# Selective scans of a four-layer vision model: where the scanned states lie, and which engine multiplies them with C

## The chip, the cores and the metric

The kernel runs on one core of a Trainium2 chip. A core has five engines that work at the same time and wait for each other through semaphores: TensorE (PE; its weight loads are listed as PEld), VectorE (DVE), ScalarE (ACT), GpSimd (POOL) and SyncE (SP), which issues the DMAs here. There are two on-chip memories, SBUF and PSUM. The metric is device time in microseconds for one execution of the whole program.

## The reference

The model has four layers on images of 64 x 64 pixels with 96 channels, batch 4. Layers 0 and 1 are state-space blocks; layers 2 and 3 are attention and feed-forward layers on tokens, and play only a side part here. The core of both blocks is a selective scan, done in four directions over the image:

```python
def step(hst, inputs):
    ul, dl, bl, cl = inputs
    dA = jnp.exp(dl[..., None] * A)
    hst = hst * dA + (dl * ul)[..., None] * bl[:, :, None, :]
    y = jnp.einsum('bkdn,bkn->bkd', hst, cl)
    return (hst, y)
h0 = jnp.zeros(u_l.shape[1:] + (A.shape[-1],), u.dtype)
_, ys = jax.lax.scan(step, h0, (u_l, delta_l, B_l, C_l))
```

For each channel there are 16 states n. Each state follows h = exp(delta A) h + (delta u) B along the sequence, and y is the sum over the 16 states of h times C. Around the scan, block 0 has a projection, a 3 x 3 depthwise convolution and SiLU before it, and a normalisation, a gate and an output projection after it; block 1 has the same between a two-dimensional Fourier transform and its inverse.

## The kernel before

**Tiling.** 128 partitions hold channels and the free dimension holds positions. The 192 channels of two images (block 0) or the 384 channels of one image (block 1) make three chunks, c = 0, 1, 2. There are six phases: two of block 0 (two images each) and four of block 1 (one image each). A phase goes through the four directions, each cut into segments: eight of 512 positions in block 0; 512, 512, 384, 384 and 320 in block 1. That makes 64 + 80 = 144 segments.

**Steps.** A segment is done in 12 steps: four quarters q of the 16 states, and in each quarter the three chunks. A step (class `Step`) scans four states, numbered j = 0 to 3 in the quarter. There are 1728 steps, listed in `steps`, and one loop (`for i, st in enumerate(steps)`) writes the instructions of all engines for a step. `tc.manual_schedule(engines=IN_ORDER)` makes TensorE, VectorE, ScalarE and GpSimd keep the order in which this loop writes them; so what stands behind a waiting instruction on its engine waits too.

**What a step needs.** For each of its four states a scan takes a factor exp(delta A) and an addend (delta u) B:

- States 0 and 1: the factors are written by ScalarE into the SBUF tile `ax` (`front_x`, line 635 through `exp`). The addends come from `bx`, which ScalarE makes with positions on the partitions (line 600, `make_bx`, given out in pieces by `Pieces.take`), and which TensorE transposes into PSUM (`transposed`, line 630).
- States 2 and 3: the factors are written by ScalarE into PSUM (`front_y`, line 635; these lines of the profile call the tile `ab`, `b` or `_l`, which is a matter of shortened names). The addends are made in SBUF by GpSimd as a product of `du` and a row of B (`front_b`, line 653).
- The PSUM tiles of both kinds come from one ring of three banks (`room`, tag `ab`).

VectorE scans (line 660). States 0 and 1 go to the SBUF tile `hx`; states 2 and 3 are scanned in place in the SBUF tile `hy`, of which there is one buffer. Each scan reads one tile in SBUF and one in PSUM. GpSimd multiplies the two states of `hx` with C in one instruction (`hcx`, line 805), VectorE those of `hy` (`hcy`, line 822). TensorE transposes each product by a matmul with the identity and adds it into a PSUM bank for the chunk (`accumulate`, line 682; 16 such matmuls a step at 512 positions), so that the sum over the 16 states is done there. After the last quarter `close_chunk` (line 709) copies the sum out and stores it.

The last column of each state is kept as the start value for the next segment (`keep_state`, line 673): for `hx` on GpSimd behind the multiply, for `hy` mostly on ScalarE.

**Loads.** The rows of B and C are broadcast over the partitions by DMAs (`broadcast`, line 580). `fetch` loads a quarter ahead, in the first chunk's step: two C tiles of two rows each from a ring of four buffers, and one B tile of two rows from a ring of two.

**Other work in the gaps.** While one segment is scanned, the next is prepared (`prepare`, with one VectorE product `du`, line 560, per segment), and the work of the other layers and images runs as generators on a queue (`Env`), some pieces per step, through `slot`. `burst` marks the places where ScalarE changes its function table (softplus, SiLU). VectorE's and GpSimd's order in a step is:

```python
scan x0; scan x1; scan y0; scan y1; hcy          # VectorE
hcx; copy of two columns; du*B for y0'; du*B for y1'   # GpSimd, ' is the next step
```

Of the kernel before, what the change touches and what calls it, by code (L numbers as in the profile page):

```python
# [456 lines left out]
class Seg:  # L457


    def __init__(self, ph, k, a, S, first, last):  # L460
# [8 lines left out]
        self.bx, self.b, self.c, self.u, self.after = {}, {}, {}, None, None  # L469


class Step:


    def __init__(self, z, q, c):
        self.z, self.q, self.c = z, q, c
        self.nm = f"{z.nm}_{q}_{c}"


def scans(tc, ctx, phases, ident):  # L480
# [92 lines left out]
    def broadcast(z, n, what):  # L573
# [3 lines left out]
        t = sp.tile([P, 2, SM], F32, name=f"bc{what}_{z.nm}_{n}", tag=f"bc{what}", bufs=2 + 2 * what)  # L577
        for i in range(NI):
            r = i * cfg.M + cfg.R + what * NST + n
            nc.sync.dma_start(  # L580
                out=t[i * PI : (i + 1) * PI, :, :S],
                in_=z.xd[r : r + 2, :S].rearrange("(o n) l -> o n l", o=1).to_broadcast([PI, 2, S]),
            )
        return t

    def fetch(z, q):
        z.c[q] = [broadcast(z, 4 * q + 2 * j, 1) for j in range(2)]
        z.b[q] = broadcast(z, 4 * q + 2, 0)
# [37 lines left out]
    def transposed(st, j):  # L626

        pb = room(st, j)
        for b, (t, n) in enumerate(st.z.blocks):
            nc.tensor.transpose(pb[:, t : t + n], st.z.bx[st.q, j][:n, b, st.c], ident[:n, :n])  # L630
        return pb
# [12 lines left out]
    def front_y(st, j):  # L644
        st.ay[j] = room(st, 2 + j)
        exp(st.ay[j][:, : st.z.S], st, 4 * st.q + 2 + j)

    def front_b(st):

        S = st.z.S  # L650
        st.hy = sp.tile([P, 2, SM], F32, name=f"hy_{st.nm}", tag="hy")
        for j in range(2):
            nc.gpsimd.tensor_tensor(  # L653
                st.hy[:, j, :S], st.z.du[:, st.c, :S], st.z.b[st.q][:, j, :S], ALU.mult
            )

    def scan(st, h, j, a, b, n):
        z = st.z
        step = -1 if z.rev else 1
        nc.vector.tensor_tensor_scan(  # L660
            h[:, j, : z.S][:, ::step],
            a[:, : z.S][:, ::step],
            b[:, : z.S][:, ::step],
# [5 lines left out]
    def keep_state(copy, st, h, n0):  # L669
        z = st.z  # L670
        if not z.last:
            e = 0 if z.rev else z.S - 1
            copy(  # L673
                z.state[st.c][:, n0 : n0 + 2].rearrange("p (j o) -> p j o", o=1), h[:, :, e : e + 1]
            )

    def accumulate(st, hc, n0):
        z = st.z
        for j in range(2):
            blocks = list(enumerate(z.blocks))  # L680
            for b, (t, n) in blocks[:: 1 - 2 * j]:
                nc.tensor.matmul(  # L682
                    z.acc[st.c][:n, b, :],
                    hc[:, j, t : t + n],
                    ident,
                    start=(n0 + j == 0 and b == 0),
                    stop=(n0 + j == NST - 1 and b == 0),
                    is_transpose=True,
                )

    def open_segment(z, before):
# [5 lines left out]
        else:  # L697
            z.state = before.state
        z.acc = [
            ps.tile([P, 512], F32, name=f"acc_{z.nm}_{c}", tag=f"acc{c}").rearrange("p (b d) -> p b d", b=NBK)  # L700
            for c in range(C)
        ]
# [17 lines left out]
    with tc.manual_schedule(engines=IN_ORDER):  # L720
        drain(prepare(segs[0]))
        drain(make_bx(segs[0], 0))
        fetch(segs[0], 0)
        st = steps[0]
        st.px, st.ay = [transposed(st, j) for j in range(2)], {}
        front_x(st)
        front_b(st)
        front_y(st, 0)
        closing = None
# [33 lines left out]
        for i, st in enumerate(steps):  # L763
            z, q, c, S = st.z, st.q, st.c, st.z.S
            nxt = steps[i + 1] if i + 1 < len(steps) else None
            if q == 0 and c == 0:
                after = z.after
                if at == 0 or z.ph is not segs[at - 1].ph:
                    if closing:
                        close_chunk(closing)  # L770
                        closing = None
# [725 lines left out]
```

## Time and profile before

| What | Value |
|---|---|
| Median of 3 runs | 11709.09 us (11697.75 to 11709.36) |
| Span of the profiled execution | 11704.4 us |
| Before the first scan | 0 to 215.5 us |
| Two phases of block 0 | 2551.9 and 2585.7 us |
| Four phases of block 1 | 1469.7, 1446.8, 1521.8 and 1516.9 us |
| Behind the last scan | 396.1 us |
| VectorE busy in these eight stretches | 111, 2420, 2436, 1306, 1295, 1427, 1410 and 143 us |
| GpSimd busy | 5, 2264, 2214, 1143, 1146, 1080, 1077 and 3 us |
| ScalarE busy | 50, 2168, 2179, 1105, 1125, 1178, 1155 and 129 us |
| TensorE busy | 123, 1967, 2099, 1251, 1236, 1201, 1184 and 239 us |
| DMA engines, mean share | 0.54, 0.50, 0.53, 0.48, 0.46, 0.36, 0.36 and 0.38 |
| Granted TensorE clock, mean | 0.88 |

How the views are read: a line of the groups gives source line, engine, operation, out<-in, shape, the count behind x, then busy microseconds and the mean nanoseconds of one, then the engine's idle time before it and what ended it. A line of the timeline gives start and length in microseconds, then the same names; `x2` means that two instructions in a row were merged into it, and the length is that of both together. A start minus the start before it is the pace of an engine, which can be less than one instruction's length, as neighbours overlap at their ends.

### The profile page before, as it was taken

The page shows a single profiled execution, that of the slowest core. Times are in us where ns is not written, and L with a number is a line of the kernel's source. Part 1 is how long each engine was busy: PE and PEld are TensorE (multiplying, and loading weights), DVE is VectorE, ACT ScalarE, POOL GpSimd, SP SyncE. Part 2 cuts the span into 40 slices and gives each one's busy share as a digit, 9 for nine tenths or more (in the row PEclk, how much of TensorE's full clock was granted, in tenths as well). Part 3 has the DMA queues.
Part 4 walks back from the last instruction along what each step waited for, and adds up shares of the span by engine and source line. Part 5 has one row for each costly group of instructions (what it writes and reads, how often), then busy time and mean ns, then how long its engine had stood idle before and what let it go on. Part 6 is the DMA issues. An engine that isn't in the chain of part 4 may idle for free. (4 is left out here: it accounts for less than half of the span.)

```text
span 11704.4 us, 164864 instructions
## 1 busy us (share of the span) xinstructions
PE 9301.7 (79%) x54800; PEld 6722.3 (57%) x54800; DVE 10549.4 (90%) x10183; ACT 9089.0 (78%) x18533; POOL 8931.5 (76%) x7075
## 2 busy tenths in 40 slices
PE   6678888787888878877888888888778877788765
PEld 3455555555666556555665565565556655565554
DVE  6899999999999998999888989988999999899974
ACT  3778888898888888887767878877787787777753
POOL 2889999887887897897768878877767767677640
PEclk8789999988988998998889989988879988898887
DMA  5454454555555445445544353454225432443242
GB/s 145 120 142 119 126 127 115 141 155 158 153 153 129 124 124 141 120 127 162 153 129 124 114 147 120 142 150 119 88 79 158 122 96 92 124 137 106 83 117 42
DMA packets 1270879, 1469.07 MB, mean 126 GB/s; under 512 B 496071, under 2 KB 1033871, under 8 KB 1260679
## 3 DMA queue, kind: packets, MB, share of 16 engines
q1 hardware_dynamic: 1270023, 1458.53, 45.5%
q8 instruction: 430, 7.05, 0.3%
q14 instruction: 426, 3.49, 0.1%
HBM read 1221.74 MB, written 236.50 MB: 125 GB/s over the span
## 5 line engine op out<-in xcount | busy, mean ns | idle before, releaser
L653 POOL TENSOR_TENSOR hy_l<-du_l,bc_l 128x512 f32<-128x512 f32 (+2 forms) x3456 | 3957.3, 1166 | 1934.8 <-DVE hcy_l L822 960.1
L805 POOL TENSOR_TENSOR hcx_l<-hx_l,bc_l 128x1024 f32<-128x1024 f32 (+2 forms) x1617 | 3525.5, 2180 | 239.1 <-DVE hx_l L660 197.9
L600 ACT ACTIVATE bx_l<-dut_l,bt_l 128x192 f32<-128x192 f32 (+2 forms) x6272 | 2793.7, 498 | 0.0
L682 PE MATMUL acc_l<-ident,hcx_l 128*128 128x128 f32 (+1 forms) x12006 | 1876.0, 305 | 392.6 <-POOL hcx_l L805 388.4
L635 ACT ACTIVATE ax_l<-delta_l,l_alog 128x512 f32<-128x512 f32 (+2 forms) x3456 | 2139.1, 667 | 0.0
L682 PE MATMUL acc_l<-ident,hcy_l 128*128 128x128 f32 (+1 forms) x12000 | 1841.9, 302 | 302.4 <-DVE hcy_l L822 299.0
L682 PEld LDWEIGHTS acc_l<-ident,hcy_l 128*128 128x128 f32 (+1 forms) x12000 | 1551.5, 155 | 859.2 <-DVE hcy_l L822 475.7
L682 PEld LDWEIGHTS acc_l<-ident,hcx_l 128*128 128x128 f32 (+1 forms) x12006 | 1526.4, 156 | 861.5 <-POOL hcx_l L805 665.9
L822 DVE TENSOR_TENSOR hcy_l<-hy_l,bc_l 128x1024 f32<-128x1024 f32 (+2 forms) x1616 | 1951.1, 1207 | 43.6
L660 DVE TENSOR_TENSOR_SCAN hx_l<-ax_l,state_l,b_l 128x512 f32<-128x512 f32 (+2 forms) x1650 | 1787.4, 1124 | 212.7 <-PE b_l L630 136.9
L660 DVE TENSOR_TENSOR_SCAN hy_l<-b_l,state_l,hy_l 128x512 f32<-128x512 f32 (+2 forms) x1649 | 1782.9, 1118 | 89.3 <-ACT b_l L635 81.4
L635 ACT ACTIVATE b_l<-delta_l,l_alog 128x512 f32<-128x512 f32 (+2 forms) x1913 | 1196.6, 628 | 627.6 <-DVE hx_l L660 599.0
L630 PE MATMUL b_l<-ident,bx_l 128*128 128x128 f32 (+1 forms) x6724 | 1169.6, 302 | 363.0 <-DVE hy_l L660 203.5
L635 ACT ACTIVATE ab_l<-delta_l,l_alog 128x512 f32<-128x512 f32 x1321 | 907.1, 689 | 547.5 <-DVE hx_l L660 496.4
L630 PEld LDWEIGHTS b_l<-ident,bx_l 128*128 128x128 f32 (+1 forms) x6724 | 827.1, 152 | 861.3 <-DVE hy_l L660 337.1
L660 DVE TENSOR_TENSOR_SCAN hy_l<-ab_l,state_l,hy_l 128x512 f32<-128x512 f32 x961 | 1172.1, 1257 | 60.8 <-POOL hy_l L653 31.9
L660 DVE TENSOR_TENSOR_SCAN hx_l<-ax_l,state_l,ab_l 128x512 f32<-128x512 f32 x962 | 1176.5, 1263 | 49.3 <-PE ab_l L630 27.3
L630 PE MATMUL ab_l<-ident,bx_l 128*128 128x128 f32 x5288 | 889.1, 305 | 383.2 <-DVE hy_l L660 206.3
L673 POOL COPY state_l<-hx_l 128x2 f32<-128x2 f32 x1344 | 1141.9, 850 | 0.0
L630 PEld LDWEIGHTS ab_l<-ident,bx_l 128*128 128x128 f32 x5288 | 652.0, 154 | 715.6 <-DVE hy_l L660 326.6
L274 PE MATMUL pc_l<-pad_l,l_dg 128*128 128x512 f32 (+2 forms) x1656 | 787.9, 564 | 56.0 <-ACT uh_l L252 46.6
L176 PE MATMUL pi_l<-xi_l,l_wi 96*128 96x384 f32 (+6 forms) x912 | 458.6, 619 | 180.0 <-ACT zh_l L342 60.4
(225 smaller groups left out, 11821.3 us busy)
## 6 DMA issues: line engine op xcount, KB each, us to landing
bc_l<-l_xd_l SPq DMA_DIRECT2D x1536, 256.0 KB
bc_l<-l_xd_l SPq DMA_DIRECT2D x384, 512.0 KB
bc_l<-l_xd_l SPq DMA_DIRECT2D x384, 384.0 KB
us_l<-l_u SPq DMA_DIRECT2D x96, 768.0 KB
l_y<-y_l SPq DMA_DIRECT2D x288, 256.0 KB
bc_l<-l_xd_l SPq DMA_DIRECT2D x192, 320.0 KB
yt_l<-l_y SPq DMA_DIRECT2D x264, 192.0 KB
yt_l<-l_y SPq DMA_DIRECT2D x128, 384.0 KB
```

The source lines that it names most:

```text
L176: self.nc.tensor.matmul(out[i * cfg.PI : (i + 1) * cfg.PI, :n], wi[:, ki, half, :], xin[:, max(i, ki), :n], start=(ki == 0), stop=(ki == c ...
L274: nc.tensor.matmul(pc[:, : n * 64].rearrange("p (r w) -> p r w", w=64), diag[:, t, :], pad[:, r - p0 + dy : r - p0 + dy + n, dx : dx + 64] ...
L600: nc.scalar.activation(t[:n, b, :, ch], z.dut[:n, b, :, ch], AF.Copy, scale=z.bt[:n, b, m : m + 1])
L630: nc.tensor.transpose(pb[:, t : t + n], st.z.bx[st.q, j][:n, b, st.c], ident[:n, :n])
L635: nc.scalar.activation(out, z.delta[:, st.c, : z.S], AF.Exp, scale=z.blk.A[:, st.c, z.k, n : n + 1])
L653: nc.gpsimd.tensor_tensor(st.hy[:, j, :S], st.z.du[:, st.c, :S], st.z.b[st.q][:, j, :S], ALU.mult)
L660: nc.vector.tensor_tensor_scan(h[:, j, : z.S][:, ::step], a[:, : z.S][:, ::step], b[:, : z.S][:, ::step], 0.0 if z.first else z.state[st.c ...
L673: copy(z.state[st.c][:, n0 : n0 + 2].rearrange("p (j o) -> p j o", o=1), h[:, :, e : e + 1])
L682: nc.tensor.matmul(z.acc[st.c][:n, b, :], hc[:, j, t : t + n], ident, start=(n0 + j == 0 and b == 0), stop=(n0 + j == NST - 1 and b == 0), ...
L805: nc.gpsimd.tensor_tensor(hcx[:, :, :S], hx[:, :, :S], z.c[q][0][:, :, :S], ALU.mult)
L822: nc.vector.tensor_tensor(hcy[:, :, :S], st.hy[:, :, :S], z.c[q][1][:, :, :S], ALU.mult)
```

## The change

Per step, state 0 is scanned in place in its PSUM tile; in the steps whose number in the segment (3q + c) leaves 1 when divided by four, state 1 is too. These states are called kept (`kept` is 1 or 2). VectorE multiplies each kept state with its row of C, from PSUM into an SBUF tile `hk`, right behind its scan, and ScalarE copies its last column. The other states (three, or two where two are kept) lie side by side in one SBUF tile `h`, of which there are three buffers. GpSimd copies their last columns in one instruction and multiplies them with C in place in one instruction, in the step that follows (`multiply(before)`), and ahead of the products for the step after it (`front_b(nxt)`). TensorE adds these in the following step as well (`add_rest(before)`). C comes as one tile of four rows from a ring of two, fetched in the second chunk's step; B as before. The chunk's PSUM sum is taken when its first kept state is added; closing a chunk and queuing a phase's side work come later accordingly.

The diff, shortened where it only renames:

```diff
...
+        self.kept = 1 + ((C * q + c) % 4 == 1)
+        self.px, self.ay = {}, {}
...
-        t = sp.tile([P, 2, SM], F32, name=f"bc{what}_{z.nm}_{n}", tag=f"bc{what}", bufs=2 + 2 * what)
+        t = sp.tile([P, many, SM], F32, name=f"bc{what}_{z.nm}_{n}", tag=f"bc{what}", bufs=2)
...
-    def fetch(z, q):
-        z.c[q] = [broadcast(z, 4 * q + 2 * j, 1) for j in range(2)]
-        z.b[q] = broadcast(z, 4 * q + 2, 0)
+    def fetch_b(z, q):
+        z.b[q] = broadcast(z, 4 * q + 2, 2, 0)
+
+    def fetch_c(z, q):
+        z.c[q] = broadcast(z, 4 * q, 4, 1)
...
     def front_y(st, j):
-        st.ay[j] = room(st, 2 + j)
-        exp(st.ay[j][:, : st.z.S], st, 4 * st.q + 2 + j)
+        st.ay[j] = room(st, j)
+        exp(st.ay[j][:, : st.z.S], st, 4 * st.q + j)
 
     def front_b(st):
 
         S = st.z.S
-        st.hy = sp.tile([P, 2, SM], F32, name=f"hy_{st.nm}", tag="hy")
+        st.h = sp.tile([P, 3, SM], F32, name=f"h_{st.nm}", tag="h", bufs=3)
         for j in range(2):
             nc.gpsimd.tensor_tensor(
-                st.hy[:, j, :S], st.z.du[:, st.c, :S], st.z.b[st.q][:, j, :S], ALU.mult
+                st.h[:, 1 + j, :S], st.z.du[:, st.c, :S], st.z.b[st.q][:, j, :S], ALU.mult
             )
 
-    def scan(st, h, j, a, b, n):
+    def scan(st, j):
         z = st.z
-        step = -1 if z.rev else 1
+        S, step, n = z.S, -1 if z.rev else 1, 4 * st.q + j
+        h = st.px[j][:, :S] if j < st.kept else st.h[:, j - 1, :S]
+        a = st.ax[:, j, :S] if j < 2 else st.ay[j][:, :S]
+        b = st.px[j][:, :S] if j < 2 else h
         nc.vector.tensor_tensor_scan(
-            h[:, j, : z.S][:, ::step],
-            a[:, : z.S][:, ::step],
-            b[:, : z.S][:, ::step],
+            h[:, ::step],
+            a[:, ::step],
+            b[:, ::step],
             0.0 if z.first else z.state[st.c][:, n : n + 1],
             ALU.mult,
             ALU.add,
         )
 
-    def keep_state(copy, st, h, n0):
+    def last(z):
+        return 0 if z.rev else z.S - 1
+
+    def multiply_kept(st, j):
+
         z = st.z
+        n = 4 * st.q + j
+        hk = sp.tile([P, SM], F32, name=f"hk_{st.nm}_{j}", tag="hk", bufs=2)
+        nc.vector.tensor_tensor(hk[:, : z.S], st.px[j][:, : z.S], z.c[st.q][:, j, : z.S], ALU.mult)
         if not z.last:
-            e = 0 if z.rev else z.S - 1
-            copy(
-                z.state[st.c][:, n0 : n0 + 2].rearrange("p (j o) -> p j o", o=1), h[:, :, e : e + 1]
+            e = last(z)
+            nc.scalar.copy(z.state[st.c][:, n : n + 1], st.px[j][:, e : e + 1])
+        accumulate(st, hk, n)
+
+    def multiply(st):
+
+        z = st.z
+        lo, n = st.kept - 1, 4 * st.q
+        h = st.h[:, lo:, : z.S]
+        if not z.last:
+            e = last(z)
+            nc.gpsimd.tensor_copy(
+                z.state[st.c][:, n + st.kept : n + 4].rearrange("p (j o) -> p j o", o=1), h[:, :, e : e + 1]
             )
-
-    def accumulate(st, hc, n0):
+        nc.gpsimd.tensor_tensor(h, h, z.c[st.q][:, st.kept :, : z.S], ALU.mult)
+
+    def accumulate(st, hc, n):
         z = st.z
-        for j in range(2):
-            blocks = list(enumerate(z.blocks))
-            for b, (t, n) in blocks[:: 1 - 2 * j]:
-                nc.tensor.matmul(
-                    z.acc[st.c][:n, b, :],
-                    hc[:, j, t : t + n],
-                    ident,
-                    start=(n0 + j == 0 and b == 0),
-                    stop=(n0 + j == NST - 1 and b == 0),
-                    is_transpose=True,
-                )
+        if n == 0:
+            z.acc[st.c] = ps.tile([P, 512], F32, name=f"acc_{z.nm}_{st.c}", tag=f"acc{st.c}").rearrange(
+                "p (b d) -> p b d", b=NBK
+            )
+        blocks = list(enumerate(z.blocks))
+        for b, (t, m) in blocks[:: -1 if n == NST - 1 else 1]:
+            nc.tensor.matmul(
+                z.acc[st.c][:m, b, :],
+                hc[:, t : t + m],
+                ident,
+                start=(n == 0 and b == 0),
+                stop=(n == NST - 1 and b == 0),
+                is_transpose=True,
+            )
+
+    def add_rest(st):
+        for j in range(st.kept, 4):
+            accumulate(st, st.h[:, j - 1], 4 * st.q + j)
...
-                        close_chunk(closing)
-                        closing = None
+                fresh = at == 0 or z.ph is not segs[at - 1].ph
+                if fresh:
                     z.ph.io["y"] = [z.blk.dram_tile(f"y{j}", (2, z.cfg.L, C * P), z.ph.g) for j in range(2)]
-                    for fn, arg in z.ph.side:
-                        E.add((fn, arg), fn(E, arg))
                 open_segment(z, segs[at - 1] if at else None)
                 if after:
                     E.require(after.ph.needs[after.k % 2])
                 pgen, pwants = prepare(after) if after else none, None
                 at += 1
+            if fresh and q == 0 and c == C - 1:
+                for fn, arg in z.ph.side:
+                    E.add((fn, arg), fn(E, arg))
             if c == 0:
                 if q + 1 < NQ:
-                    fetch(z, q + 1)
+                    fetch_b(z, q + 1)
                 elif after:
                     drain(pgen)
                     more = Pieces(after, 0, 4)
-                    fetch(after, 0)
-            hx = sp.tile([P, 2, SM], F32, name=f"hx_{st.nm}", tag="hx")
-            scan(st, hx, 0, st.ax[:, 0], st.px[0], 4 * q)
-            front_y(st, 1)
+                    fetch_b(after, 0)
+            if c == 1:
+                if q + 1 < NQ:
+                    fetch_c(z, q + 1)
+                elif after:
+                    fetch_c(after, 0)
+            scan(st, 0)
+            front_y(st, 2)
             if nxt:
-                nxt.ay = {}
                 front_x(nxt)
+            multiply_kept(st, 0)
+            front_y(st, 3)
             long = burst()
-            scan(st, hx, 1, st.ax[:, 1], st.px[1], 4 * q + 1)
+            if before:
+                multiply(before)
+            if nxt:
+                front_b(nxt)
             slot(None)
+            scan(st, 1)
+            if st.kept > 1:
+                multiply_kept(st, 1)
             if nxt:
                 if c == C - 1:
                     drain(more.gen)
...
                         more = Pieces(z, q + 2, 6)
                     elif q + 1 == NQ:
                         more = Pieces(nxt.z, 1, 6)
-                nxt.px = [transposed(nxt, 0)]
-            hcx = sp.tile([P, 2, SM], F32, name=f"hcx_{st.nm}", tag="hcx", bufs=2)
-            nc.gpsimd.tensor_tensor(hcx[:, :, :S], hx[:, :, :S], z.c[q][0][:, :, :S], ALU.mult)
-            keep_state(nc.gpsimd.tensor_copy, st, hx, 4 * q)
+                transposed(nxt, 0)
             more.take(skip=long)
-            scan(st, st.hy, 0, st.ay[0], st.hy[:, 0], 4 * q + 2)
+            scan(st, 2)
+            slot(None, hold=long)
             if nxt:
-                nxt.px.append(transposed(nxt, 1))
-            slot(None, hold=long)
-            scan(st, st.hy, 1, st.ay[1], st.hy[:, 1], 4 * q + 3)
-            keep_state(nc.gpsimd.tensor_copy if long else nc.scalar.copy, st, st.hy, 4 * q + 2)
-            if nxt:
-                front_y(nxt, 0)
-            more.take(skip=long and c == C - 1)
+                transposed(nxt, 1)
             if closing:
                 close_chunk(closing)
-            accumulate(st, hcx, 4 * q)
+            closing = None
+            if before:
+                add_rest(before)
+                closing = before if before.q == NQ - 1 else None
+            scan(st, 3)
+            more.take(skip=long and c == C - 1)
             slot(LATE)
-            hcy = sp.tile([P, 2, SM], F32, name=f"hcy_{st.nm}", tag="hcy", bufs=2)
-            nc.vector.tensor_tensor(hcy[:, :, :S], st.hy[:, :, :S], z.c[q][1][:, :, :S], ALU.mult)
-            if nxt:
-                front_b(nxt)
-            accumulate(st, hcy, 4 * q + 2)
-            closing = st if q == NQ - 1 else None
-        close_chunk(closing)
+            before = st
+        if closing:
+            close_chunk(closing)
+        multiply(before)
+        add_rest(before)
+        close_chunk(before)
```

More of the change, by code (lines that the diff above doesn't have):

```diff
@@ L468, in __init__ @@
         self.runs = [(0, full, P)] + ([(full, full + 1, S % P)] if S % P else [])
-        self.bx, self.b, self.c, self.u, self.after = {}, {}, {}, None, None
+        self.bx, self.b, self.c, self.acc, self.u, self.after = {}, {}, {}, {}, None, None
 class Step:
@@ L571, in prepare, with broadcast @@
                 nc.scalar.copy(z.dut[:n, lo:hi, c], pt[:n, lo:hi, :])
-    def broadcast(z, n, what):
+    def broadcast(z, n, many, what):
         cfg, S = z.cfg, z.S
         NI, PI = cfg.NI, cfg.PI
-        t = sp.tile([P, 2, SM], F32, name=f"bc{what}_{z.nm}_{n}", tag=f"bc{what}", bufs=2 + 2 * what)
+        t = sp.tile([P, many, SM], F32, name=f"bc{what}_{z.nm}_{n}", tag=f"bc{what}", bufs=2)
         for i in range(NI):
@@ L581, in broadcast @@
                 out=t[i * PI : (i + 1) * PI, :, :S],
-                in_=z.xd[r : r + 2, :S].rearrange("(o n) l -> o n l", o=1).to_broadcast([PI, 2, S]),
+                in_=z.xd[r : r + many, :S].rearrange("(o n) l -> o n l", o=1).to_broadcast([PI, many, S]),
             )
         return t
-    def fetch(z, q):
-        z.c[q] = [broadcast(z, 4 * q + 2 * j, 1) for j in range(2)]
-        z.b[q] = broadcast(z, 4 * q + 2, 0)
+    def fetch_b(z, q):
+        z.b[q] = broadcast(z, 4 * q + 2, 2, 0)
+    def fetch_c(z, q):
+        z.c[q] = broadcast(z, 4 * q, 4, 1)
     def make_bx(z, q):
@@ L626, in transposed @@
     def transposed(st, j):
-        pb = room(st, j)
+        pb = st.px[j] = room(st, j)
         for b, (t, n) in enumerate(st.z.blocks):
             nc.tensor.transpose(pb[:, t : t + n], st.z.bx[st.q, j][:n, b, st.c], ident[:n, :n])
-        return pb
     def exp(out, st, n):
@@ L698, in open_segment @@
             z.state = before.state
[L699 to L702, printed above, removed]
     def close_chunk(st):
@@ L722, in scans @@
         drain(make_bx(segs[0], 0))
-        fetch(segs[0], 0)
+        fetch_b(segs[0], 0)
+        fetch_c(segs[0], 0)
         st = steps[0]
-        st.px, st.ay = [transposed(st, j) for j in range(2)], {}
+        for j in range(2):
+            transposed(st, j)
         front_x(st)
         front_b(st)
-        front_y(st, 0)
-        closing = None
+        before = closing = None
         more, pgen, pwants, at, due = Pieces(segs[0], 1, 4), none, None, 0, 0.0
@@ L767, in scans @@
                 after = z.after
-                if at == 0 or z.ph is not segs[at - 1].ph:
-                    if closing:
-                        close_chunk(closing)
-                        closing = None
+                fresh = at == 0 or z.ph is not segs[at - 1].ph
+                if fresh:
                     z.ph.io["y"] = [z.blk.dram_tile(f"y{j}", (2, z.cfg.L, C * P), z.ph.g) for j in range(2)]
-                    for fn, arg in z.ph.side:
-                        E.add((fn, arg), fn(E, arg))
                 open_segment(z, segs[at - 1] if at else None)
```

## The prediction

> **What bounds the kernel now.** I read the page's first part, then the groups of VectorE (DVE) and GpSimd (POOL) with shapes kept apart, then the timeline of these two engines in one undisturbed stretch of block 0.
>
> ```profile
> PE 9301.7 (79%) x54800; PEld 6722.3 (57%) x54800; DVE 10549.4 (90%) x10183; ACT 9089.0 (78%) x18533; POOL 8931.5 (76%) x7075
> ...
> L653 POOL TENSOR_TENSOR hy_l<-du_l,bc_l 128x512 f32<-128x512 f32 x2304 | 2882.4, 1272 | 1170.3 <-DVE hcy_l L822 590.7 <-ACT state_l L673 150.7 <-issue 133.1
> L805 POOL TENSOR_TENSOR hcx_l<-hx_l,bc_l 128x1024 f32<-128x1024 f32 x1152 | 2721.9, 2363 | 126.9 <-DVE hx_l L660 114.3 <-issue 5.7 <-POOL hy_l L653 1.6
> L673 POOL COPY state_l<-hx_l 128x2 f32<-128x2 f32 x1344 | 1141.9, 850 | 0.0
> L822 DVE TENSOR_TENSOR hcy_l<-hy_l,bc_l 128x1024 f32<-128x1024 f32 x1152 | 1510.2, 1311 | 32.1
> ```
>
> By busy time VectorE bounds, with GpSimd well behind. The timeline says more:
>
> ```profile
> 1522.99 2.50 POOL L653 TENSOR_TENSOR hy_l<-du_l,bc_l 128x512 f32<-128x512 f32 x2
> 1525.45 2.37 POOL L805 TENSOR_TENSOR hcx_l<-hx_l,bc_l 128x1024 f32<-128x1024 f32 x1
> 1527.77 1.18 POOL L673 COPY state_l<-hx_l 128x2 f32<-128x2 f32 x1
> 1529.05 2.51 POOL L653 TENSOR_TENSOR hy_l<-du_l,bc_l 128x512 f32<-128x512 f32 x2
> ```
>
> ```profile
> 1522.93 2.33 DVE L660 TENSOR_TENSOR_SCAN hx_l<-ax_l,ab_l 128x512 f32<-128x512 f32 x2
> 1525.18 2.31 DVE L660 TENSOR_TENSOR_SCAN hy_l<-ab_l,hy_l 128x512 f32<-128x512 f32 x2
> 1527.52 1.38 DVE L822 TENSOR_TENSOR hcy_l<-hy_l,bc_l 128x1024 f32<-128x1024 f32 x1
> 1528.98 2.33 DVE L660 TENSOR_TENSOR_SCAN hx_l<-ax_l,ab_l 128x512 f32<-128x512 f32 x2
> ```
>
> GpSimd has no gap in this step. Its copy of two columns lasts 1.18 us, and ends when VectorE's `hcy` multiply ends (1528.90); elsewhere the same copy takes 0.20 us. So VectorE's multiply of two SBUF tiles and a GpSimd instruction exclude each other, and the step is one chain of both engines: 2.46 (initial products) + 2.32 (`hcx`) + 1.28 (copy, waiting for `hcy`) = 6.06 us. The median step of block 0, from scan to scan, is 6.2 us. The scans overlap GpSimd's multiplies freely: each reads one SBUF tile and one PSUM tile.
>
> Does a VectorE multiply with one operand in PSUM exclude GpSimd too? The normalisation shows it:
>
> ```profile
> 5439.03 1.85 DVE L421 TENSOR_TENSOR yb_l<-yb_l,pm_l 128x512 f32<-128x512 f32 x3
> ...
> 5439.24 2.37 POOL L805 TENSOR_TENSOR hcx_l<-hx_l,bc_l 128x1024 f32<-128x1024 f32 x1
> 5441.54 0.20 POOL L673 COPY state_l<-hx_l 128x2 f32<-128x2 f32 x1
> ```
>
> Two of the three subtractions start inside GpSimd's 2.37 us and neither engine is slowed. The kept states' multiply has that form.
>
> **The change, part by part.** There are 1728 steps: 1152 of 512 columns, 384 of 384, 192 of 320. The sum is made on the profiled execution, 11704.4 us (the runs' median 11709.09 lies 4.7 above).
>
> *VectorE.* Out: all `hcy`, 1510.2 + 310.7 + 130.1 + 69.6 + 33.7 = 2054 us in the groups of L822. In: 15 kept multiplies in 12 steps, 2160 in all. Nearest rows are L421's subtractions, 0.673 us at 512 and 0.542 at 384, so about 0.477 at 320: 1440 x 0.673 + 480 x 0.542 + 240 x 0.477 = 1344 us. A multiply behind the scan that feeds it starts 1.29 us after that scan, a scan behind an independent scan 1.175 us (spacing of starts): 0.115 us for each such pair, and there are 2160 instead of 1728, so +50. VectorE: -660 us.
>
> [...]
>
> *Scans in place in PSUM*, 2160 of them. No row has a scan that writes PSUM. ScalarE's exponentials take 0.708 us into SBUF (`ax`) and 0.688 into PSUM (`ab`): below, -0.02 us each, -43 us. Above, reading and writing one bank could take turns and double a scan's 1.175 us: +2300 us. I take 0; the scans already read that bank at the speed of the other pair (1.264 against 1.257 us).
>
> *GpSimd.* Spacing of starts: 1.23 us for 512 elements, 2.32 for 1024, so 3.41 for 1536. Three states in three steps of four, two in the fourth: 0.75 x 3.41 + 0.25 x 2.32 = 3.14. With 2.46 for the initial products and 0.26 for an unblocked copy in seven steps of eight: 5.83 against 6.06, -0.23 us. The same from the rows of 384 and 320 columns: 4.49 against 4.68, 3.84 against 4.00. 1152 x 0.23 + 384 x 0.19 + 192 x 0.16 = 369 us. In place and with three columns I take the same rate; the bounds are -0 and +0.2 us a step (a second copy's worth), +350 us.
>
> *What sets the step.* If GpSimd alone does: 11704 - 369 = 11335. If VectorE does, with its old idle time: 11704 - 660 = 11044. GpSimd's products for step i+1 now come after the multiply of step i-1, and three `h` tiles replace one `hy`; so the waits for `hcy` go (960.1 us of GpSimd in the table of waits). From its multiply to the scan that needs its next product to the end of that step is 0.26 + 3.14 + 1.23 + 2.4 = 7.0 us for two steps of 5.8: some 4 us of slack where there was none. That lets GpSimd stay busy through ScalarE's bursts (4.1 us: softplus 1.49 and two table loads of 1.28). I take 120 of the 291 us between the ends, under half, because VectorE and GpSimd would be nearly equal in each step and ScalarE gets more to do.
>
> [...]
>
> *ScalarE.* 2160 one-column copies in 5 of 6 segments, 1800 x 0.19 = 342 us, for 1285 of 0.19, 244 us: +98 us, hidden while it is busy 2168 of 2552 us in the first phase; without that cover +98. Each waits for scan 0; queued behind it are the exponential for scan 3 and the `bx` pieces. That exponential now also waits for the kept multiply, whose bank it takes: VectorE is then 1.9 us into the step and needs it at 4.3, against 0.69 for the exponential.
>
> *TensorE.* As many transposes and accumulations, 24 a step. The kept accumulation waits for the multiply, with side matmuls and the next transpose behind it, and that transpose waits for scan 1 anyway. The other 12 wait for GpSimd's multiply; behind them stand side work and the next step's accumulation, and GpSimd's next product waits for the `h` tile they free, two steps later. 0 taken.
>
> *SyncE and DMAs.* C comes in one tile of four rows, fetched a step later, with the same bytes. Its issue waits for GpSimd's multiply of the last step of the quarter before; behind it in SP's order stand the side loads and `y` stores. One fetch is 1 MB, about 4.5 us at the 230 GB/s of a burst, needed two steps (12 us) later less GpSimd's lag of up to 5: covered. Uncovered by 1 us it would cost 576 x 1. Closing a chunk and queuing side work come a step or two later: +4 us at the end.
>
> Sum: 11704.4 - 369 - 120 + 4 + 4.7 = 11224, so **11220 us**.
>
> **Rivals.**
> 1. *ScalarE becomes the bound in block 0.* It is busy 0.85 of those phases and waits in order on VectorE. If it can't pass 0.87: (2168 + 22) / 0.87 = 2517 for 2552, 2530 for 2586, -91 us; block 1 keeps its share of 369, -192. 11704 - 283 + 9 = 11430. For it: its waits on `hx` (599.0 + 496.4 us). Against: these are waits for the engine that gets faster.
> 2. *The slack also absorbs stalls.* VectorE is idle some 695 us between the first scan and the last; half gone from VectorE's end: 11044 - 350 + 9 = 10700. Against: much of that idle time is ScalarE's and TensorE's lateness.
> 3. *Slower: scans in PSUM cost more.* Doubled, 1440 x 1.175 + 480 x 0.908 + 240 x 0.775 = 2314 us on VectorE: 11044 + 2314 = 13360. It decides from 660 / 2160 = 0.31 us a scan. Nothing in the trace speaks for it, nor excludes it.
> 4. *Slower: the kept multiply still excludes GpSimd.* 2160 at L421's spacing (0.60, 0.47, 0.41) is 1190 us: 11335 + 1190 = 12520. L421's rows speak against it.
>
> **How the numbers follow.** Forecast 0.58 (11080 to 11350 alone); rival 1 0.17; rival 2 0.10; rival 3 0.09; rival 4 0.04; gains that cancel to nothing 0.02. Faster by over 0.2%, which is about what a measurement here can tell from no change: 0.85; within it 0.02; slower 0.13. The range, 10880 to 11580, leaves out most of rival 2 and the slower cases.
>
> **What would show it.** Kept scans at 1.25 us; `hk` at 0.67; the three-column copy near 0.2, not 1.18; GpSimd's multiply of 1536 near 3.45; block 0's median step 5.8 to 5.95; VectorE's busy time near 9890. The forecast fails if kept scans pass 1.5 us, if GpSimd's copies or products still stretch to the end of a kept multiply, or if ScalarE is busy without gaps.

## The result

The changed kernel takes 12123.99 us (median of 4 runs, 12118.23 to 12150.53), the kernel before 11709.23 us on the same chip (4 runs, 11697.75 to 11731.81). The ratio is 1.0353, 95% interval 1.0335 to 1.037: slower by 415 us, where the forecast of 11220 lay 489 us below. The profiled execution spans 12127.0 us against 11704.4.

From the page of the changed kernel, busy time of each engine (share of the span, number of instructions):

```profile
PE 9227.8 (76%) x54800; PEld 6811.3 (56%) x54800; DVE 10388.1 (86%) x10615; ACT 9096.0 (75%) x19048; POOL 9553.1 (79%) x6920
```

VectorE (DVE) did get less to do: 161 us less than before. The forecast said 660 less. The groups of the changed kernel with shapes kept apart (busy us, mean ns of one, then the idle time ahead of them and what ended it):

```profile
L699 POOL TENSOR_TENSOR h_l<-h_l,bc_l 128x1536 f32<-128x1536 f32 x864 | 3009.8, 3484 | 185.2 <-DVE h_l L666 126.8 <-POOL state_l L696 0.2
L656 POOL TENSOR_TENSOR h_l<-du_l,bc_l 128x512 f32<-128x512 f32 x2304 | 2955.5, 1305 | 362.8 <-PE acc_l L709 283.8 <-DVE du_l L562 66.2 <-issue 9.3
...
L666 DVE TENSOR_TENSOR_SCAN ab_l<-ax_l,state_l,ab_l 128x512 f32<-128x512 f32 x639 | 813.9, 1274 | 133.7 <-PE ab_l L634 132.8
...
L683 DVE TENSOR_TENSOR hk_l<-ab_l,bc_l 128x512 f32<-128x512 f32 x848 | 586.4, 692 | 38.5 <-issue 9.4
...
L696 POOL COPY state_l<-h_l 128x3 f32<-128x3 f32 x1044 | 330.2, 316 | 615.8 <-DVE h_l L666 601.9 <-DMA bc_l<-l_xd_l 10.6 <-DVE qb L1129 0.5
...
L1245 DVE TENSOR_SCALAR h<-h,b 128x512 f16<-128x512 f16 x192 | 183.1, 996 | 11.6 <-ACT h L1242 8.3
...
L573 ACT COPY dut_l<-pp_l 128x512 f32<-128x512 f32 x288 | 168.6, 586 | 365.2 <-PE pp_l L570 365.0
```

The prices of the new instructions are near what the prediction took: a kept scan 1.274 us, a kept multiply 0.692, GpSimd's (POOL) multiply of 1536 elements 3.48, its three-column copy 0.32, so mostly unblocked. The last two lines are instructions that the change does not touch. The feed-forward's bias and maximum (L1245, L1211 before) takes 996 ns, and ScalarE's (ACT) copies of the transposed `du` wait 365 us for TensorE. The same two groups before:

```profile
L571 ACT COPY dut_l<-pp_l 128x512 f32<-128x512 f32 x288 | 166.3, 578 | 128.2 <-PE pp_l L568 127.8
...
L1211 DVE TENSOR_SCALAR h<-h,b 128x512 f16<-128x512 f16 x192 | 64.9, 377 | 14.2 <-ACT h L1208 10.7
```

Where the time lies, by phase, from the first scan of each to the next one's (us; idle time is gaps of over 0.15 us; the expectations call the six phases stretches):

| | block 0 | | block 1 | | | |
|---|---|---|---|---|---|---|
| length before | 2552 | 2586 | 1470 | 1447 | 1522 | 1517 |
| length after | 2530 | 2608 | 1495 | 1494 | 1699 | 1685 |
| VectorE's side work before | 24 | 57 | 57 | 47 | 210 | 197 |
| VectorE's side work after | 26 | 81 | 77 | 68 | 371 | 357 |
| VectorE idle before | 112 | 120 | 149 | 136 | 82 | 95 |
| VectorE idle after | 254 | 279 | 228 | 232 | 152 | 153 |

Side work is what neither scans nor multiplies with C nor makes `du`: gates, attention, feed-forward, most of it in the last two phases. It is 388 us longer, and VectorE's idle time grows from 694 to 1298 us. Of this idle time TensorE ended 317 us before and 722 after, ScalarE 294 and 494, GpSimd 68 and 50, DMAs 16 and 20. Both have to be explained.

**The longer side work.** Instruction by instruction, those with two SBUF inputs, and the single-input ones of the feed-forward and the layer norm, grew where they begin inside a GpSimd multiply (the 32 of line 266 never do, and kept their 2.35 us); those with an operand in PSUM and the reductions did not. Means in the changed kernel, inside and outside a GpSimd multiply: two SBUF inputs, 2.77 and 0.74 us at line 440 (512 columns) and 2.35 and 0.56 at line 1268; one input, 1.81 and 0.96 for the feed-forward's cast of line 1248; an operand in PSUM, 0.74 and 0.74 at line 435 (512 columns) and 0.68 and 0.68 at line 421. The timeline of VectorE and GpSimd in the fifth phase of the changed kernel (start, us for all of a row, engine, line, operation):

```profile
8447.92 1.26 DVE L666 TENSOR_TENSOR_SCAN h_l<-ab_l,state_l,h_l 128x512 f32<-128x512 f32 x1
...
8448.70 1.28 POOL L656 TENSOR_TENSOR h_l<-du_l,bc_l 128x512 f32<-128x512 f32 x1
...
8449.10 4.75 DVE L1245 TENSOR_SCALAR h<-h,b 128x512 f16<-128x512 f16 x3
...
8449.91 0.27 POOL L696 COPY state_l<-h_l 128x3 f32<-128x3 f32 x1
...
8450.26 3.44 POOL L699 TENSOR_TENSOR h_l<-h_l,bc_l 128x1536 f32<-128x1536 f32 x1
...
8453.65 3.25 POOL L656 TENSOR_TENSOR h_l<-du_l,bc_l 128x512 f32<-128x512 f32 x2
8453.88 1.90 DVE L1248 CAST h<-h 128x1536 fp8e5<-128x1536 f16 x1
8455.70 1.28 DVE L666 TENSOR_TENSOR_SCAN ab_l<-ax_l,state_l,ab_l 128x512 f32<-128x512 f32 x1
```

The first row in which they meet is L1245: three bias instructions last 4.75 us. The third began at 8450.31, 0.05 us after GpSimd's multiply, and ended at 8453.84, 0.15 us after it. Of all 192 in the kernel, 90 begin inside a GpSimd multiply and take 1.73 us on the mean; the other 102 take 0.35. Before, 42 begin inside one and take 0.49, 150 take 0.34: the slot for side work then stood behind both scans of `hy`, when 0.34 us of GpSimd's `hcx` multiply were left on the mean and never more than 0.73, and then GpSimd copied or waited for `hcy`. In the changed kernel GpSimd begins its longest instruction there (46 of the 90 begin inside line 699's multiply, 44 inside a product of `du` and B). Summed over all VectorE side work and `du`, the instructions of these kinds are 427 us longer.

The reductions of the layer norm take 0.93 to 0.95 us inside and outside GpSimd's multiplies. What the two engines wait over, no trace here shows: the expectations below call it the port, which stands for these waits and nothing more.

### The profile page after: what moved, and what is told of

The parts are those of the page before. It is cut to its first block, busy times and chain, and to the rows that moved or that the text cites. A ratio compares the mean times of both kernels' runs of the same rounds, so it can differ in the third digit from the quotient of the medians.

```text
span 12127.0 us, 163448 instructions
## 1 busy us (share of the span) xinstructions
PE 9227.8 (76%) x54800; PEld 6811.3 (56%) x54800; DVE 10388.1 (86%) x10615; ACT 9096.0 (75%) x19048; POOL 9553.1 (79%) x6920
## 5 line engine op out<-in xcount | busy, mean ns | idle before, releaser
L699 POOL TENSOR_TENSOR h_l<-h_l,bc_l 128x1536 f32<-128x1536 f32 (+2 forms) x1728 | 5037.2, 2915 | 395.9 <-DVE h_l L666 267.1
L656 POOL TENSOR_TENSOR h_l<-du_l,bc_l 128x512 f32<-128x512 f32 (+2 forms) x3456 | 4079.5, 1202 | 644.9 <-PE acc_l L709 531.0
L709 PE MATMUL acc_l<-ident,h_l 128*128 128x128 f32 x17424 | 2579.1, 303 | 103.6 <-POOL h_l L699 102.0
L709 PEld LDWEIGHTS acc_l<-ident,h_l 128*128 128x128 f32 x17424 | 2305.6, 159 | 147.6 <-POOL h_l L699 128.6
L666 DVE TENSOR_TENSOR_SCAN h_l<-b_l,state_l,h_l 128x512 f32<-128x512 f32 (+2 forms) x1692 | 1844.2, 1119 | 230.5 <-ACT b_l L638 169.9
L666 DVE TENSOR_TENSOR_SCAN b_l<-ax_l,state_l,b_l 128x512 f32<-128x512 f32 (+2 forms) x1056 | 1192.2, 1129 | 317.8 <-PE b_l L634 315.2
L666 DVE TENSOR_TENSOR_SCAN h_l<-ab_l,state_l,h_l 128x512 f32<-128x512 f32 x1020 | 1257.3, 1264 | 129.1 <-ACT ab_l L638 83.9
L709 PE MATMUL acc_l<-ident,k_l 128*128 128x128 f32 (+1 forms) x4258 | 757.9, 299 | 600.3 <-DVE k_l L683 589.7
L696 POOL COPY state_l<-h_l 128x3 f32<-128x3 f32 x1392 | 400.8, 288 | 879.0 <-DVE h_l L666 857.1
L709 PE MATMUL acc_l<-ident,hk_l 128*128 128x128 f32 x3392 | 585.3, 300 | 552.0 <-DVE hk_l L683 539.0
L666 DVE TENSOR_TENSOR_SCAN ab_l<-ax_l,state_l,ab_l 128x512 f32<-128x512 f32 x639 | 813.9, 1274 | 133.7 <-PE ab_l L634 132.8
```

The costliest lines, as they stand in the source:

```text
L656: nc.gpsimd.tensor_tensor(st.h[:, 1 + j, :S], st.z.du[:, st.c, :S], st.z.b[st.q][:, j, :S], ALU.mult)
L666: nc.vector.tensor_tensor_scan(h[:, ::step], a[:, ::step], b[:, ::step], 0.0 if z.first else z.state[st.c][:, n : n + 1], ALU.mult, ALU.add,)
L696: nc.gpsimd.tensor_copy(z.state[st.c][:, n + st.kept : n + 4].rearrange("p (j o) -> p j o", o=1), h[:, :, e : e + 1])
L699: nc.gpsimd.tensor_tensor(h, h, z.c[st.q][:, st.kept :, : z.S], ALU.mult)
L709: nc.tensor.matmul(z.acc[st.c][:m, b, :], hc[:, t : t + m], ident, start=(n == 0 and b == 0), stop=(n == NST - 1 and b == 0), is_transpose ...
```

## The experiments

All times are medians, and the ratios are to the kernel before, which ran side by side on the same chip (11703 to 11722 us there). The four groups below ran on four chips, so a difference of some 15 us between two of them says nothing; the ratios are safer. Each edit is one to the changed kernel unless said otherwise.

### First: four single causes

**The banks.** The prediction took it that the exp for scan 3 goes to the bank that state 0 leaves, as in the kernel before. In the built program of the changed kernel that is so in 725 of 1728 steps; in 149 it goes to the bank that state 2's scan is still reading.

```diff
-        return ps.tile([P, 512], F32, name=..., tag="ab", bufs=3)
+        banks[0] += 1
+        return ps.tile([P, 512], F32, name=..., tag=f"ab{banks[0] % 3}")
```

> The changed kernel with one edit: the three PSUM banks of the scans are taken in a fixed turn (three names, one bank each) instead of by the pool's own choice. In the built program of the changed kernel the pool gives the exp of state 3 the bank that state 2's scan is still reading in 149 of 1728 steps (111 of them at the tenth step of a segment), and the bank of state 1 in 767; in the kernel before it is the bank of state 0 in all 1728. Theory A (banks: the exp of state 3 waits for scan 2, which shows as the exact wait of 0.83 us ahead of scan 3, 99 times in block 0): 11820 to 11990 us, the 0.83 us waits gone, the tenth step of a segment in block 0 from 7.5 to 6.2-6.9 us. Theory B (the loss is VectorE's other instructions waiting for GpSimd, longer by 427 us in sum): 12100 to 12150, no change. Theory C (TensorE's and ScalarE's order, whatever the banks): 12050 to 12130.

Measured: 12167.3 us, ratio 1.038 (1.0362 to 1.0397). No gain, and in no theory's range, though the exp for scan 3 now has state 0's bank in all 1728 steps, as the prediction took it. The waits of exactly 0.83 us, 81 ahead of scan 3 and 18 ahead of scan 2 in the first two phases, are gone but for three, and most other steps are shorter, but the sixth step of a segment went from 6.2 to 8.5 us in block 0. Such a step in its timeline:

```profile
1290.47 1.28 ACT L546 ACT_TABLE_LOAD   x1
1290.71 0.69 DVE L686 TENSOR_TENSOR k_l<-b_l,bc_l 128x512 f32<-128x512 f32 x1
1291.32 2.45 DVE L669 TENSOR_TENSOR_SCAN h_l<-b_l,state_l,h_l 128x512 f32<-128x512 f32 x2
...
1291.77 1.48 ACT L546 ACTIVATE delta_l<-delta_l 128x1536 f32<-128x1536 f32 x1
1293.27 1.28 ACT L547 ACT_TABLE_LOAD   x1
...
1294.57 0.16 ACT L689 COPY state_l<-b_l 128x1 f32<-128x1 f32 x1
...
1294.78 1.21 PE L637 MATMUL b_l<-ident,bx_l 128*128 128x128 f32 x8 [2.66 <-ACT state_l L689]
...
1295.54 1.29 DVE L669 TENSOR_TENSOR_SCAN b_l<-ax_l,state_l,b_l 128x512 f32<-128x512 f32 x1 [1.77 <-PE b_l L637]
```

In a fixed turn the next step's first transpose takes the bank of state 1. Where state 1 is kept, its last column is copied by ScalarE, and that copy stands behind softplus and its two table loads. The pool's choice had walked round this place and made others.

**TensorE's order.** `add_rest(before)` and the line that sets `closing` moved from ahead of `scan(st, 3)` to behind `slot(LATE)`.

> The changed kernel with one edit: TensorE's accumulation of GpSimd's states stands behind the step's last slot instead of ahead of scan 3, so that transposes and side matmuls do not stand behind the end of GpSimd's multiply. Theory C (TensorE in order behind GpSimd, then ScalarE behind TensorE: ScalarE waits 533.6 us in all for the du transposes against 204.9 before): 11950 to 12050 us, that wait back to 200-350 us. Theory A (banks): 12090 to 12130, since the pool still gives the bank of state 2 in 128 steps. Theory B (VectorE waits for GpSimd): 12100 to 12150.

Measured: 12084.92, ratio 1.0312 (1.0297 to 1.0327): 39 us won, in no theory's range. ScalarE's wait for the `du` transposes fell from 534 to 379 us, short of theory C's 200 to 350, and little of that reached the time. The first two phases gained nothing (2537 and 2618 us), the last two are 22 and 18 us shorter.

**The bias on ScalarE.**

```diff
-                nc.vector.tensor_scalar(h16[:, j, :], h16[:, j, :], q["b1"][:, j : j + 1], 0.0, ALU.add, ALU.max)
+                nc.scalar.activation(h16[:, j, :], h16[:, j, :], AF.Relu, bias=q["b1"][:, j : j + 1])
```

> The changed kernel with one edit: the feed-forward's add of the bias with maximum (192 instructions of VectorE, 996 ns each now, 377 ns in the kernel before) is a Relu of ScalarE. Theory B (VectorE's other instructions wait for GpSimd, the larger part of the loss): the 191 us leave VectorE, the last two of the six stretches are shorter by 60 to 95 us each, 11940 to 12010 us in all. Theory C (in-order waits of ScalarE and TensorE are the larger part): ScalarE gets some 110 us more (about 0.57 us each, from its 512-column copies) ahead of its exps, so little is won: 12050 to 12140. Theory A (banks): 12050 at the least, since the instructions' own price was 72 us.

Measured: 12089.68, ratio 1.0316 (1.0301 to 1.0331). VectorE's side work fell by 85 and 87 us in the last two phases, but the cast behind it then waited for ScalarE, so they are only 17 and 31 us shorter:

```profile
L1246 DVE CAST h<-h 128x1536 fp8e5<-128x1536 f16 x64 | 95.9, 1498 | 183.4 <-ACT h L1245 183.2
```

Of these 183 us of idle time 143 lie in the last two phases; without the edit this cast never waits for ScalarE. By its time the run sides with theory C, but the wait is one that the edit itself put in; a later run issues the Relu earlier.

**GpSimd's multiply, state by state.**

```diff
-        nc.gpsimd.tensor_tensor(h, h, z.c[st.q][:, st.kept :, : z.S], ALU.mult)
+        for j in range(4 - st.kept):
+            nc.gpsimd.tensor_tensor(h[:, j], h[:, j], z.c[st.q][:, st.kept + j, : z.S], ALU.mult)
```

> [...] Theory B (VectorE's port instructions wait for the end of a GpSimd instruction): their mean wait falls by half or more (the feed-forward bias from 996 to 550-750 ns), 11880 to 12020 us. Theory A and C (banks, order): GpSimd pays about 0.1 us a step for the more instructions and TensorE waits no less: 12110 to 12250.

Measured: 12051.46, ratio 1.0286 (1.0266 to 1.0305). The bias group of this kernel:

```profile
L1246 DVE TENSOR_SCALAR h<-h,b 128x512 f16<-128x512 f16 x192 | 118.9, 660 | 12.7 <-ACT h L1243 9.4
```

93 of them still begin inside a GpSimd multiply, and now take 1.00 us instead of 1.73. The last two phases are 81 and 75 us shorter though GpSimd has more instructions; the first two, where there is little side work, are 60 and 27 us longer (GpSimd 2404 us busy instead of 2315). Same instructions on VectorE, shorter GpSimd multiplies (1.30 us each at 512 columns, where one of 1536 took 3.48), shorter waits: theory B holds for side work, with a time between its range and the other's.

### Second: order mended, then the waits for GpSimd

**Banks and burst.** The fixed turn, and `long = burst()` moved behind the second `multiply_kept`.

> The changed kernel with two edits: the fixed turn of the three banks (as in ring_fixed), and the burst of Softplus or SiLU on ScalarE placed behind the second kept product of a step instead of ahead of it. Theory D (a fixed turn is right, but the state copy of the second kept state then stands behind the burst on ScalarE, keeps its bank, and the next step's first transpose with it, so the seventh step's scan 0 waits 2.23 us): the sixth step in block 0 from 8.5 to 6.2-6.6 us, 64 times in block 0 and 80 in block 1, so 11830 to 11960 us. Theory B (the loss is the port alone): 12090 to 12170. Theory C (in-order waits move from one place to the next): the sixth or seventh step stays above 7.5 us, 12050 to 12170.

Measured: 11998.44, ratio 1.024 (1.0225 to 1.0256): 126 us won, somewhat short of theory D's range. The sixth step is back at 6.2 us, as D said.

**All of the order.** Besides, `rest_late`'s move, and the drain of the next segment's preparation later in its step:

```diff
                 elif after:
-                    drain(pgen)
-                    more = Pieces(after, 0, 4)
                     fetch_b(after, 0)
...
                 transposed(nxt, 0)
+            if c == 0 and q + 1 == NQ and after:
+                drain(pgen)
+                more = Pieces(after, 0, 4)
             more.take(skip=long)
```

> ring_burst with two edits more: the drain of the next segment's preparation (du transposes and their copies) stands behind the exps of its step instead of ahead of its first scan, and TensorE's accumulation of GpSimd's states stands at the step's end (as in rest_late). Theory C and D (order of TensorE and ScalarE): the tenth step in block 0 from 7.1 to 6.2-6.5 us, the first two stretches 2330 to 2430 us each (from 2530 and 2608), 11560 to 11760 us in all. Theory B (port): under 60 us faster than ring_burst.

Measured: 11847.18, ratio 1.0113 (1.0095 to 1.0132). The order gives back 277 us, and even the upper end of theory C's range lies 87 us too low: it had the first phase at 2330 to 2430 us, and it took 2477. What the drain did at the tenth step, in the timeline of the changed kernel:

```profile
1311.13 0.59 ACT L573 COPY dut_l<-pp_l 128x512 f32<-128x512 f32 x1 [1.15 <-PE pp_l L570]
...
1311.67 1.26 DVE L666 TENSOR_TENSOR_SCAN b_l<-ax_l,state_l,b_l 128x512 f32<-128x512 f32 x1
...
1312.23 1.47 PE L709 MATMUL acc_l<-ident,h_l 128*128 128x128 f32 x12
...
1313.54 0.60 PE L570 MATMUL pp_l<-ident,du_l 128*128 128x128 f32 x4
...
1314.17 0.59 ACT L573 COPY dut_l<-pp_l 128x512 f32<-128x512 f32 x1 [2.46 <-PE pp_l L570]
...
1314.66 0.70 ACT L638 ACTIVATE b_l<-delta_l,l_alog 128x512 f32<-128x512 f32 x1
...
1315.28 1.32 ACT L638 ACTIVATE ax_l<-delta_l,l_alog 128x512 f32<-128x512 f32 x2
1315.49 1.27 DVE L666 TENSOR_TENSOR_SCAN h_l<-b_l,state_l,h_l 128x512 f32<-128x512 f32 x1
...
1316.80 0.69 ACT L638 ACTIVATE b_l<-delta_l,l_alog 128x512 f32<-128x512 f32 x1 [0.15 <-DVE h_l L666]
...
1317.59 1.28 DVE L666 TENSOR_TENSOR_SCAN h_l<-b_l,state_l,h_l 128x512 f32<-128x512 f32 x1 [0.83 <-ACT state_l L686]
```

Scan 0 starts at 1311.67, but ScalarE is still in the last copies of `du`, which wait for transposes that stand on TensorE behind twelve accumulations of GpSimd's states. All exps of the step come some 2.5 us late. In this step the exp for scan 3 has the bank of state 2 as well, so it waits for scan 2 to end, and scan 3 waits 0.83 us for it. (The exp ended at 1317.49 and scan 3 began at 1317.59; the view names the state copy that ScalarE does behind the exp.) With the order mended this step takes 6.19 us. Median length of the 12 steps of a segment, first phase (us):

```
before        6.14 6.14 6.22 6.20 6.29 6.22 6.28 7.85 6.21 6.17 6.21 6.14
after         5.52 6.76 5.45 5.85 5.84 6.22 7.10 7.86 5.46 7.54 5.46 5.45
ring_fixed    5.45 6.20 5.44 5.45 5.64 8.52 5.47 7.85 5.46 7.13 5.47 5.44
order_all     5.46 6.20 5.44 5.44 5.45 6.19 6.09 8.35 5.46 6.19 5.44 5.44
```

**Order and waits.** To `order_all`, two edits more: the Relu of `relu_scalar` put behind its copy, a slot ahead of the cast, and the multiply state by state in the last two phases alone.

> [...] Theory B for what order leaves: each of the last two stretches 140 to 200 us shorter than in order_all (75 to 81 were won by the split alone, 17 to 31 by the ScalarE bias with its wait in place), 11200 to 11450 us in all. Theory C: the gain beside order_all is under 100 us, because GpSimd or ScalarE then ends the steps.

Measured: 11684.83, ratio 0.9973 (0.9962 to 0.9984). The last two phases took 1532 and 1548 us against 1626 and 1627, so 93 and 80 less, not 140 to 200. The whole gain over `order_all` is 162 us, between the two theories' numbers. The version is faster than both kernels, by 0.27% than the one before. What remains, from its page:

```profile
PE 9120.0 (78%) x54800; PEld 6695.1 (57%) x54800; DVE 10139.7 (87%) x10423; ACT 9287.2 (79%) x19240; POOL 9637.3 (82%) x7760
```

In the first phase GpSimd is busy 2311 of 2473 us, VectorE 2270, ScalarE 2167: none has much to spare.

**The same Relu in the kernel before.**

> The kernel before, with the feed-forward's bias and maximum on ScalarE right behind its copy. Theory B: in the kernel before these 192 instructions cost VectorE 377 ns each and wait for nobody, so at most their 72 us are won, 11630 to 11720 us. If it wins more than 100 us, the edit is a gain of its own and not a sign of the port.

Measured: 11737.78, ratio 1.002 (1.0011 to 1.003). By itself it loses 28 us there, so the Relu is no gain of its own.

### Third: without GpSimd's multiply

`multiply(before)` keeps its copy and loses its `tensor_tensor`, once in the changed kernel and once in `order_all`. Both leave out the product of GpSimd's states with C.

> The changed kernel without GpSimd's in-place multiply with C (the states 1 to 3, or 2 and 3, are added to the result without their product with C): GpSimd keeps 2.5 us of 6 a step, so no end of GpSimd and few port holds are left, while the banks and the order of TensorE and ScalarE stay as they are. Theory B and E (port, and GpSimd's own end at 93% of the first stretches once the order is mended): 11450 to 11650 us, the feed-forward bias below 600 ns. Theory C (banks and in-order waits that GpSimd's end has no part in): 11700 to 11900.

> order_all without GpSimd's in-place multiply with C (the same part left out). Theory E (with the order mended, GpSimd's time and its port are what is left): 11100 to 11350 us, the first stretch 2330 to 2400 us against 2477, the last two 1430 to 1520 against 1626. Theory F (VectorE and ScalarE, not GpSimd, end the steps): over 11550.

Measured: 11500.58 (ratio 0.9814, 0.9794 to 0.9834) and 11236.17 (0.9588, 0.9569 to 0.9608). With 12124 and 11847 this makes a square: taking out the multiply is worth 623 and 611 us, mending the order 277 and 264. The two add up, neither hides the other. The bias instruction is back at 0.36 to 0.37 us on the mean; side work and `du` of VectorE are 422 us shorter in the first pair. By phase that is 154 and 151 us where the last two phases are 167 and 158 shorter, but 34 and 36 where the first two are 111 and 90 shorter. If all of it counts in the time, two thirds of the 623 are VectorE's waits for GpSimd; `relu_scalar` warns that it need not. The rest would be GpSimd's late end and what waits for it, which no run separates.

**One kept state.** `order_port` with `kept` = 1 in all steps of the last two phases.

> order_port with one state kept in every step of the last two stretches, instead of two in every fourth: VectorE loses 60 products of 0.5 to 0.7 us and their 60 state copies of ScalarE in each stretch, GpSimd gets 60 columns' worth of 0.8 to 1.2 us more. Theory F (VectorE with its side work ends these stretches: 1386 and 1398 us busy of 1532 and 1548, GpSimd 1298 and 1289): 20 to 50 us faster than order_port, 11630 to 11670. Theory E (GpSimd and its port): 10 to 60 us slower, 11690 to 11750.

Measured: 11682.8, ratio 0.9969 (0.9957 to 0.9982): the same. VectorE 15 and 26 us less busy, GpSimd 62 and 64 more. Moving these states from one engine to the other changes nothing there, and neither theory's number came.

### Last: the parts of the order

> The changed kernel with one edit of the two in ring_burst: the burst behind the second kept product, the banks as the pool gives them. Theory A (the banks matter beside the burst): 12080 to 12140 us, since 141 steps keep the shared bank. Theory G (the burst alone brings what ring_burst won, banks are of no account): 11970 to 12030.

> The changed kernel with one edit of order_all: the drain of the next segment's preparation behind the exps of its step. In the built program the pool then shares the bank of states 2 and 3 in 43 steps instead of 149. Theory C (the tenth step waits for ScalarE, which waits for the du transposes): the tenth step in block 0 from 7.5 to 6.2-6.6 us, 144 such steps, 11930 to 12020 us in all. Theory G (the drain only moves the wait to the next step): 12080 to 12130.

> order_all with the banks as the pool gives them (shared in 35 steps, the bank of state 1 for state 3's exp in 857). Theory A (the fixed turn is a part of the gain): 40 to 120 us slower than order_all, 11890 to 11970. Theory G (order alone): 11830 to 11870.

Measured: 12088.25 (1.0325, 1.031 to 1.0341), 11971.22 (1.0225, 1.021 to 1.024) and 11932.47 (1.019, 1.0173 to 1.0207). The burst alone wins 36, the drain 153, and the late accumulation won 39. All three lie in the ranges of the theories that gave these parts a share (A, C and A). With the order mended, the fixed turn is worth another 85 (11932 to 11847), while alone it lost 32 (by the ratios) to 43, hardly clear of the noise. The drain's edit also changes what the pool gives (43 shared steps instead of 149), so its 153 are not the drain alone.

## Why the prediction was wrong

**VectorE, -660: the step that failed first.** The multiplies that left and came were priced right (0.692 against 0.673 us), and scans in PSUM were rightly taken at 0: a kept scan takes 0.01 us more than one that writes SBUF (1.274 against 1.264). But the term counted only the instructions that the diff names. Side work and `du` stayed in it at their old durations, and they grew by 427 of the 499 us that are missing between -660 and -161. The prediction saw the conflict with GpSimd in one form, VectorE's multiply of two SBUF tiles, which the change removes. That was a misreading: the rows looked at held that form alone, but the trace before has the conflict in others too. The bias took 0.49 us instead of 0.34 in its 42 cases, and `du` 2.00 us in the 82 of these 96 that begin inside a GpSimd multiply, 1.73 in the other 14, which the group's mean hides:

```profile
L560 DVE TENSOR_TENSOR du_l<-delta_l,us_l 128x1536 f32<-128x1536 f32 x96 | 188.3, 1962 | 37.1 <-DMA bc_l<-l_xd_l 37.1
```

The change put GpSimd's 3.48 us where such instructions stand. The instructions that paid were ones that were not moved. With -161 in the place of -660, VectorE's end by the prediction's own sum is 11543, later than GpSimd's 11335. That would still have been faster than before; the rest of the miss is idle time.

**"TensorE ... 0 taken", and ScalarE's copies "hidden": the second.** Prices and counts were right; what failed is that in-order engines were costed by what is added to them. VectorE's idle time that TensorE ended is 405 us longer than before, and that which ScalarE ended 200 us. The accumulations of GpSimd's states came between the `du` transposes and ScalarE's copies, the bank of a kept state was tied to a copy behind a burst, and the exp's bank was assumed to be state 0's. The four edits to these places won 277 us together. They brought the part that ScalarE ends back to 312 us, from 494, but the part that TensorE ends only to 660, from 722.

**The slack of 4 us, and 120 us for it.** It was not there to take: GpSimd's copies waited 602 us for VectorE's scans (L696 above). It was counted for GpSimd's products alone. State 2's exp now stands behind scan 0 of its own step, where the kernel before had it at the end of the step before; that this shorter lead lets ScalarE's lateness through to VectorE fits VectorE's idle time, but was not tried by itself. Span less busy time grew from 1155 to 1739 us, where the forecast's sum implies 1329 (11219 less 9890 busy).

**GpSimd, -369.** Undisturbed steps of 5.44 us where one state is kept and 6.20 where two are show that the chain of GpSimd and `hcy` is gone, as said. GpSimd's rates were right: in the first phase, where it does not wait, its starts lie 3.41 us apart for 1536 elements and 1.23 for 512 (medians), as forecast. But the median step there is 6.19, not 5.8 to 5.95, and 5.99 in `order_all`. GpSimd is then busy 93% of that phase, some 6.0 us a step. That it bounds there is likely and not shown: taking out its multiply made the phase 127 us shorter, of which VectorE's side work and `du` are 47.

**The rivals.** None was it. ScalarE as the bound comes nearest, and only as lateness: it is busy 2150 of 2530 us. TensorE's lateness, the larger part of the new idle time, was no rival at all. The loads were covered, as said: DMAs ended 20 us of VectorE's idle time. The kept multiply does not exclude GpSimd: 0.69 us inside and outside its multiplies. That the mended kernel without GpSimd's multiply takes 11236 us, near the 11220 forecast, is chance: the sum had GpSimd's work in it, but not what this work does to its neighbours.

**What stays open.** Why VectorE still waits 660 us for TensorE in `order_all`, 517 of them ahead of scan 0, against 317 in the kernel before. How the pool comes to its choice of banks, and what of `drain_only`'s 153 us is banks. The granted clock was 0.87 in the changed kernel and 0.88 in the one before; TensorE's busy time fell even so (9301.7 to 9227.8 us), but what the clock does to the waits was not separated. Giving the state copies of kept states to another engine, or moving `du` to a place where GpSimd is short, was not tried; `du` grew from 1.96 to 2.83 us in the mended version.

## What to carry to other kernels

When a conflict between two engines shows in one instruction, look at every other instruction of these engines inside and outside the long ones of the other, and ask what each will meet after the change; one that is not in the diff may pay most: here such instructions grew by 427 us. Removing a wait that paced two engines also moves where the long instruction of the one stands under the short ones of the other: here 90 of the 192 bias instructions began inside a GpSimd multiply, where 42 had before. After a change of buffers, look at which buffer each tile got, not at how many there are.

## What the runs showed of the hardware

A VectorE instruction that waited for GpSimd counted as busy: the wait lay within its own duration, and the bias, where it began inside a GpSimd multiply, ended 0.15 us behind it (median of 90). So a longer mean at an unchanged shape was the sign of it (996 ns against 377 for the bias). Even a tensor-scalar of 128 x 8 elements went from 0.17 to 1.46 us when it began inside a GpSimd multiply, while the kept multiply of 512 columns, with one operand in PSUM, took 0.69 us in the 1231 cases that did and in the 209 that did not.
